# A four-layer graph network on one core: layers 1 and 2 computed over half the columns at a time, and the end of layer 0 moved behind the branch, block by block

## The chip, the cores and the metric

The kernel runs on one core of one Trainium2 chip. The metric is the device time of one execution in microseconds (us). A core has five engines that run their own instruction streams and wait for each other through semaphores: TensorE (PE in the profile; its weight loads are PEld), VectorE (DVE), ScalarE (ACT), GpSimd (POOL) and SyncE (SP), which here issues nearly all loads. Sixteen DMA engines move data between memory (HBM) and the on-chip memory SBUF. TensorE writes its results into PSUM, from where VectorE or ScalarE fetch them.

## The reference

There are N = 2708 nodes with D = 128 features, `x`, and one dense adjacency `adj` of 2708 x 2708 zeros and ones in float32, 29.3 MB. Four layers each take `h = max(layernorm(x), 0)` and add a graph operation to `x`. Cut to what matters:

```python
# layer 0: attention
H = h @ weight.T
Tau = adj.T * exp(max(0.2 * C, C))            # C[i, j] = alpha_src[j] + alpha_dst[i]
x = x + (adj.T * (Tau / Tau.sum(1))) @ H
# layer 1: normalised convolution
adj_hat = adj + eye(n);  d = (adj_hat.sum(1) + 1e-8) ** -0.5
x = x + relu((d[:, None] * adj_hat * d[None, :]) @ h @ weight)
# layer 2: mean aggregation, batch norm over all nodes
agg = adj.T @ h / deg
g = agg @ W_n.T + b_n + h @ W_c.T + b_c
x = x + relu(gamma * (g - g.mean(0)) * rsqrt(g.var(0) + 1e-5) + beta)
# layer 3: two products with adj around an attention of low rank
```

Layers 1 and 2 are each, in the main, one product of the whole adjacency with a 2708 x 128 matrix. In layer 2 the mean and variance over all nodes must be known before the layer can be added to `x`.

## The kernel before

**Tiling.** The 2708 nodes make T = 22 tiles of 128 rows (the last has 20), and the columns of the adjacency make NB = 6 blocks of 512 (the last has 148), listed in `E0`; `TILES[b]` gives the four row tiles that correspond to block b. `xs`, `hn`, `hs` hold node features by tiles; `hT` and `yT` hold a features-by-nodes matrix; `row_a`, `row_b` and `dflat` (two times N wide) are large scratch rows, [128, N] each.

**Layer 0** (up to L394) runs over the 22 row tiles of `adj`. After the loop come the flag (L362 to L368), the denominators `rden`, and a loop over the six blocks (L380 on): the last two tiles' matmuls, `evacuate` of the accumulator into `hT`, transposes back to tiles, an addition into `xs`, and `layernorm(b, hn, dis)`, which makes layer 1's input `hn`. `layernorm` takes statistics on VectorE, a power -0.5 on GpSimd (L165), scale and shift on VectorE, and the rectified output on ScalarE (L183). During layer 0, at `t == T - 4`, the first two row tiles of `adj_t` for layer 1 are loaded into `dflat`.

**The branch.** The flag tells whether all inputs of the adjacency have empty low halves. Each engine reads it and goes into one of two copies of `rest(exact, stack3)`; here it is `exact=True`. Whatever stands ahead of the branch is finished by an engine before it goes in. At the head of `rest` GpSimd writes the reciprocal degrees `rdeg` to DRAM element by element (L464) and reads them back spread over all partitions into `row_a` (L465), which layer 2's end uses.

**Exact products.** A float32 operand goes to TensorE in the format F32R. The features are cut into a high and a low part, `h_hi` and `h_lo` (`cut_in_two`, L481 and L482), so each adjacency row tile is used by two matmuls per block. The row tile itself is copied once to F32R (L503) by ScalarE or VectorE, into the pool `ring` (four whole rows).

**`loader`** hands out row tiles: load i goes into the buffer `turn[i % len(turn)]`. Layer 1 has five whole-row buffers (two halves of `dflat`, `row_b`, `hT`, and one of pool `raws`), layer 2 has four (`dflat` twice, `hn`, `raws`). A load can be issued when the copy to `ring` that last read its buffer is done; SP issues in order.

**`product`** runs one layer: for each of the first 18 row tiles, all six blocks are accumulated in six PSUM banks (`aggregate`, L216, 12 matmuls a tile); the last four tiles are loaded and worked off block by block, with `finish` behind each block. Layer 1's `finish1` takes one block out of PSUM, multiplies by the weight (L534), rectifies (L536), adds into `xs` and runs `layernorm(b, h2)` and `cut_in_two(h2, b)`, where `h2` is layer 2's input. Layer 2's `finish2` makes the two products of the layer in float32 (L567, L568) and block statistics (`st2`, L570). During layer 2's first loads `load_with_turn` transposes `h2` block by block into `hT`. Behind the last block `bn_aggr` joins the statistics (L574), and layer 2's end and layer 3 follow.

The program says what depends on what; a scheduler puts the instructions of each engine in one order. `keep_in_program_order` ties the instructions that are marked with it to their order in the text.

Of the kernel before, what the change touches and what calls it, by code (L numbers as in the profile page):

```python
# [14 lines left out]
ALU = mybir.AluOpType  # L15
# [4 lines left out]
def kernel(  # L20
# [35 lines left out]
    TILES = [range(c // P, min(c // P + 4, T)) for c, _ in E0]  # L56
    CUT = 3 * 512

    NLAST = 4

    def rows(t):
        return min(P, N - t * P)

    def fill(a, src, t):

        if rows(t) < P:
            nc.gpsimd.memset(a, 0.0)
        nc.sync.dma_start(a[: rows(t), :], src[t * P : t * P + rows(t), :])
        return a

    def cols(t):
# [13 lines left out]
    def bank():  # L85
        return ps.tile([P, 512], F32, tag="bank", name="bank")
# [100 lines left out]
    def turned(p, src, tiles, flat=None):  # L187

        for q, t in enumerate(tiles):
            nc.tensor.transpose(p[:, cols(q)], src[:, cols(t)] if flat else src[:, t, :], ident)  # L190
# [19 lines left out]

    def aggregate(stationary, moving, accs, start, stop, blocks=range(NB)):
        parts = stationary if isinstance(stationary, list) else [stationary]
        for b in blocks:
            lo, hi = E0[b]
            for i, w in enumerate(parts):
                nc.tensor.matmul(  # L216
                    accs[b][:, : hi - lo],
                    w,
                    moving[:, lo:hi],
                    start=start and i == 0,  # L220
                    stop=stop and i == len(parts) - 1,
                )

    def product(order, stationary, load, blocks, finish, extra=None):

        accs = [acc_bank(b) for b in range(NB)]
        for i, t in enumerate(order[:-NLAST]):
            a = load(t)
            aggregate(stationary(t), a, accs, i == 0, False)
            if extra:  # L230
                extra(t, accs)
        last = [(t, load(t)) for t in order[-NLAST:]]
        for b in blocks:
            for t, a in last:
                if extra and t in TILES[b]:
                    extra(t, accs)
                aggregate(stationary(t), a, accs, False, t == order[-1], [b])
            finish(b, accs[b])

    with ExitStack() as stack:  # L240
# [72 lines left out]
        for t in range(T):  # L313
            a = first_rows[t] if t < 3 else load_rows(adj, t)
            late = t >= T - 2
            rhs = (yT, row_b)[t % 2]
            for h, (h0, h1) in enumerate(((0, CUT), (CUT, N))):
                w = h1 - h0
# [32 lines left out]
            if t == T - 4:  # L351

                for i in range(2):
                    fill(dflat[:, i * N : (i + 1) * N], adj_t, i)
            if t == 10:
# [104 lines left out]
    def rest(exact, stack3):  # L460
# [26 lines left out]
        def loader(src, fixed, there=0):  # L487

            turn = [*fixed, raws] + ([] if exact else [ring] * NLAST)
            count = [0]  # L490

            def load(t):
                i = count[0]
                count[0] += 1
                a = turn[i % len(turn)]
                if a is raws or a is ring:
                    a = a.tile([P, N], F32, tag="rows", name="rows")
                if i >= there:
                    fill(a, src, t)
# [3 lines left out]
                m = nc.scalar.copy(r, a) if i % 2 else nc.vector.tensor_copy(r, a)  # L503
# [8 lines left out]
        def load_plus_one(t):  # L512
            a = next_row(t)
            if not exact:
                r = rows(t)
                nc.vector.tensor_add(a[:r, vcols(t)], a[:r, vcols(t)], ident[:r, :r])
            return a

        def plus_one(t, accs):

            r = rows(t)
            o = t % 4 * P
            for part_h in halves_of(hn)(t):
                nc.tensor.matmul(accs[t // 4][:, o : o + r], part_h, ident_r[:, :r], start=False, stop=False)

        for b in range(NB):
            cut_in_two(hn, b)
        def finish1(b, acc):
            evacuate(b, yT, acc)
# [19 lines left out]
        tot = small.tile([P, 8], F32, tag="tot", name="tot", bufs=1)  # L549
        turns = list(range(NB))  # L550

        next_row2 = loader(adj, [*two, hn.rearrange("p t d -> p (t d)")[:, :N]])

        def load_with_turn(t):
            a = next_row2(t)
            if turns:
                b = turns.pop(0)
# [3 lines left out]
            return a  # L561

# [700 lines left out]
```

## Time and profile before

| | |
|---|---|
| median of 3 runs | 898.41 us (897.56 to 898.52) |
| profiled execution | span 898.0 us, 8549 instructions, mean TensorE clock 0.922 of full speed |
| PE busy | 743.5 us (83%) |
| DVE busy | 581.6 us (65%) |
| ACT busy | 529.0 us (59%) |
| POOL busy | 194.6 us (22%) |
| DMA | 218.57 MB, mean 243 GB/s over the span |
| layer 0 | start to about 200 us |
| layer 1, first to last aggregation matmul | 234.8 to 322 us |
| layer 2, first aggregation matmul to `bn_aggr` | 335.6 to 409.7 us |

A line of a timeline gives start, length, engine, line and operation, what is written from what, its shape, how many in a row, and in brackets how long the engine sat idle before it and what released it ("issue": nothing that the profile shows). A line of a table of stretches gives the stretch, its length, the busy time of PE, PEld, DVE, ACT and POOL with the number of instructions, the granted TensorE clock (1.00 is full), the mean busy share of the 16 DMA engines and the GB/s that they moved. A line of the chain gives start, length and the piece of work that was waited for.

### The profile page before, as it was taken

The numbers are of one execution on the slowest core, as the hardware profiler recorded it, in microseconds if no ns is written. First come the engines' busy times: TensorE is split into PE (matmuls) and PEld (weight loads), VectorE is DVE, ScalarE is ACT, GpSimd is POOL, SyncE is SP. The second block draws the span as 40 slices with busy tenths as digits, with TensorE's granted clock in tenths as the row PEclk, the third lists the DMA queues.
The fourth block names the chain that finished last, engine by engine and source line by source line (L and its number), as shares of the span: only waits on it lengthen the run. The fifth ranks groups of instructions, "written<-read, shape, count | busy, mean of one in ns | idle before, by whom it ended". The sixth has DMA issues, their size and how long they took to land.

```text
span 898.0 us, 8549 instructions
## 1 busy us (share of the span) xinstructions
PE 743.5 (83%) x2980; PEld 430.8 (48%) x2980; DVE 581.6 (65%) x1079; ACT 529.0 (59%) x569; POOL 194.6 (22%) x159
## 2 busy tenths in 40 slices
PE   3599999991578869887767988389999999989996
PEld 2333333330466747764422322255555555545784
DVE  5599888885422472236886987366676666764844
ACT  3999999984234463345791015277777877766100
POOL 3000000022001020011100011365666666620010
PEclk9799999995699969997887999589999999999999
DMA  8154645404599929976510893576777777785993
GB/s 324 63 186 161 234 176 180 178 10 162 112 424 395 357 113 406 422 296 270 173 56 1 344 415 128 214 282 249 281 287 277 270 264 267 276 306 220 419 421 121
DMA packets 33394, 218.57 MB, mean 243 GB/s; under 512 B 4458, under 2 KB 13338, under 8 KB 13866
## 3 DMA queue, kind: packets, MB, share of 16 engines
q1 hardware_dynamic: 21596, 150.19, 43.5%
q0 software_dynamic: 8656, 65.76, 20.2%
q10 hardware_dynamic: 3090, 1.99, 0.7%
q8 instruction: 26, 0.43, 0.2%
q14 instruction: 26, 0.21, 0.1%
HBM read 214.12 MB, written 3.79 MB: 243 GB/s over the span
## 4 chain that ended last, share of the span: by engine, by line
DMA 22%; PE 19%; DVE 13%; POOL 7%; issue 7%; ACT 6%; DVEq 0%; POOLq 0%; ACTq 0%
DMA dflat<-in_adj_t_dram 6%; DMA dflat<-in_adj_dram 6%; PE bank L1141 5%; DMA hs<-in_adj_t_dram 4%; PE acc L1085 3%; PE acc L760 3%; PE acc L216 3%; DMA row_b<-pre_d,pre_i 2%; DMA yT<-pre_d,pre_i 2%; ACT rows L1103 2%; DVE rows L503 2%; POOL hs L597 2%; POOL hT L597 2%; PE bank L1031 1%; POOL row_b L597 1%
## 5 line engine op out<-in xcount | busy, mean ns | idle before, releaser
L1141 PE MATMUL bank<-rows,d_hi 128*128 128x512 f32 (+1 forms) x264 | 108.3, 414 | 36.9 <-DVE d_hi L1110 17.4
L216 PE MATMUL acc<-rows,h_hi 128*128 128x512 f32 (+1 forms) x264 | 104.2, 400 | 31.5 <-DVE rows L503 21.6
L1085 PE MATMUL acc<-e,xw 128*128 128x512 f32 (+1 forms) x264 | 104.3, 545 | 0.0
L1146 ACT ACTIVATE ln<-bank,tiny 128x512 f32<-128x512 f32 x132 | 79.9, 633 | 34.8 <-PE bank L1141 34.8
L1141 PE MATMUL bank<-rows,d_lo 128*128 128x512 f32 (+1 forms) x264 | 100.4, 391 | 0.0
L216 PE MATMUL acc<-rows,h_lo 128*128 128x512 f32 (+1 forms) x264 | 97.4, 386 | 0.0
L1141 PEld LDWEIGHTS bank<-rows,d_hi 128*128 128x128 f32 x264 | 52.6, 199 | 65.3 <-ACT ln L1146 29.4
L1149 DVE TENSOR_TENSOR e<-e,ln 128x1536 f32<-128x1536 f32 (+2 forms) x66 | 69.7, 1096 | 20.1 <-ACT ln L1146 19.9
L324 DVE SCALAR_TENSOR_TENSOR tau<-tau,e_hi,a 128x1536 f32<-128x1536 f32 (+1 forms) x44 | 70.6, 1622 | 7.3 <-DMA a<-in_adj_dram 5.0
L216 PEld LDWEIGHTS acc<-rows,h_hi 128*128 128x128 f32 x264 | 51.8, 197 | 45.7 <-DVE rows L503 22.6
L1085 PEld LDWEIGHTS acc<-e,xw 128*128 128x128 f32 x264 | 48.4, 190 | 52.6 <-issue 52.6
L321 ACT ACTIVATE tau<-row_a,e_neg,e_lo 128x1536 f32<-128x1536 f32 (+1 forms) x44 | 65.7, 1505 | 2.9 <-PE bank L333 2.7
L333 PE MATMUL bank<-tau,ones_at 128*32 128x512 f32 (+1 forms) x264 | 53.0, 567 | 8.3 <-DVE tau L324 8.3
L216 PEld LDWEIGHTS acc<-rows,h_lo 128*128 128x128 f32 x264 | 51.8, 196 | 10.8 <-issue 1.0
L1155 ACT ACTIVATE e<-e 128x2708 f32<-128x2708 f32 x22 | 54.2, 2462 | 4.2 <-DVE e L1149 4.2
L503 ACT CAST rows<-dflat 128x2708 fp32r<-128x2708 f32 x11 | 27.0, 2452 | 50.0 <-DMA dflat<-in_adj_t_dram 28.3
L1141 PEld LDWEIGHTS bank<-rows,d_lo 128*128 128x128 f32 x264 | 52.7, 200 | 7.4
L216 PE MATMUL acc<-yT,hs 128*128 128x512 f32 x132 | 56.3, 560 | 0.0
L216 PE MATMUL acc<-row_b,hs 128*128 128x512 f32 x132 | 56.1, 558 | 0.0
L216 PE MATMUL acc<-rows,y_hi 128*128 128x512 f32 x132 | 49.3, 380 | 5.2 <-DVE rows L1218 3.3
L503 DVE CAST rows<-dflat 128x2708 fp32r<-128x2708 f32 x11 | 17.3, 1570 | 54.5 <-DMA dflat<-in_adj_t_dram 30.3
L216 PE MATMUL acc<-rows,y_lo 128*128 128x512 f32 x132 | 47.7, 376 | 0.0
(406 smaller groups left out, 1404.2 us busy)
## 6 DMA issues: line engine op xcount, KB each, us to landing
a<-in_adj_dram SPq DMA_DIRECT2D x21, 1354.0 KB
rows<-in_adj_t_dram SPq DMA_DIRECT2D x21, 1354.0 KB
dflat<-in_adj_t_dram SPq DMA_DIRECT2D x15, 1354.0 KB
dflat<-in_adj_dram SPq DMA_DIRECT2D x11, 1354.0 KB
hT<-in_adj_t_dram SPq DMA_DIRECT2D x9, 1354.0 KB
row_b<-in_adj_t_dram SPq DMA_DIRECT2D x8, 1354.0 KB
hn<-in_adj_dram SPq DMA_DIRECT2D x5, 1354.0 KB
rows<-in_adj_dram SPq DMA_DIRECT2D x5, 1354.0 KB
```

The source lines that it names most:

```text
L216: nc.tensor.matmul(accs[b][:, : hi - lo], w, moving[:, lo:hi], start=start and i == 0, stop=stop and i == len(parts) - 1,)
L321: nc.scalar.activation(tau[:, :w], row_a[:, h0:h1], AF.Relu, bias=e_neg[:, t : t + 1], scale=e_lo[:, t : t + 1])
L324: nc.vector.scalar_tensor_tensor(tau[:, :w], tau[:, :w], e_hi[:, t : t + 1], a[:, h0:h1], ALU.add, ALU.mult)
L333: nc.tensor.matmul(den[g : g + 32, : hi - lo], ones_at[:, b // GR, :], tau[:, lo - h0 : hi - h0], start=(t == 0 and b < GR), stop=(t == T ...
L503: m = nc.scalar.copy(r, a) if i % 2 else nc.vector.tensor_copy(r, a)
L597: return nc.gpsimd.indirect_dma_start(out=out, out_offset=None, in_=src, in_offset=bass.IndirectOffsetOnAxis(ap=idx, axis=0),)
L760: nc.tensor.matmul(accs[b][64 * h : 64 * h + 2 * NC, : hi - lo], wts[:r, t, :], a[:r, lo:hi], start=(t == 0), stop=(t == T - 1),)
L1085: m = nc.tensor.matmul(accs[b][:, : hi - lo], xw, e[:, lo:hi], start=(s == 0), stop=(s == NE - 1))
L1141: m = nc.tensor.matmul(num[:, : hi - lo], d, a[:, lo:hi], start=(i == 0), stop=(i == len(products) - 1))
L1146: nc.scalar.activation(ln[:, lo:hi], num[:, : hi - lo], AF.Ln, bias=tiny)
L1149: tc.keep_in_program_order(nc.vector.tensor_sub(e[:, beg:hi], e[:, beg:hi], ln[:, beg:hi]))
L1155: tc.keep_in_program_order(nc.scalar.activation(e, e, AF.Exp))
```

## The change

Layers 1 and 2 go over the columns in two passes, `COLS`: blocks 0 to 2 (1536 columns), then blocks 3 to 5 (1172 columns). `product_by_halves` takes the place of `product` for both: in each pass it loads the half rows of all 22 tiles, accumulates three blocks, and finishes the three blocks behind the last four tiles. Both layers take the tiles in plain order. Loads are `fill_half`, each marked to stay in program order. Layer 1 has eight half-row buffers (three in `dflat`, one in `row_b`, four in `raws`), layer 2 also eight (`hn` in place of `row_b`); `ring` has six half rows. `hT` is no longer a load buffer in layer 1. Three half rows of `adj_t` are loaded during layer 0.

Of layer 0's last loop only the matmuls and `evacuate` stay ahead of the branch. The transposes, the addition, the layernorm and the cut of a block are now `finish0(b)`, behind the branch: block 0 ahead of layer 1's product, blocks 1 to 5 called with the loads of tiles 0, 4, 8, 12 and 16 of the first pass. `rden` moves to a pool that lives on. The cut of `h2` for blocks 0 to 2 is called in layer 1's second pass (after the loads 5, 9 and 13), for block 3 and for blocks 4 and 5 in `finish1`. The transposes of `h2` are called in layer 2 after loads 2, 4 and 6 of each pass. The copies to `ring` alternate between ScalarE and VectorE as before, except that loads 0 to 4 of a layer all go to ScalarE.

```diff
+    COLS = ((0, CUT), (CUT, N))
...
+    def fill_half(a, src, t, h):
+
+        if rows(t) < P:
+            nc.gpsimd.memset(a, 0.0)
+        tc.keep_in_program_order(
+            nc.sync.dma_start(a[: rows(t), :], src[t * P : t * P + rows(t), slice(*COLS[h])])
+        )
...
+    def product_by_halves(order, stationary, load, finish, extra, after):
+
+        for h, (h0, _) in enumerate(COLS):
+            blocks = range(3 * h, 3 * h + 3)
+            accs = {b: acc_bank(b) for b in blocks}
+            for i, t in enumerate(order[:-NLAST]):
+                a = load(t, h)
+                aggregate(stationary(t), a, accs, i == 0, False, blocks, h0)
+                if t // 4 in blocks:
+                    extra(t, accs)
+                after(i, h)
+            last = [(t, load(t, h)) for t in order[-NLAST:]]
+            for b in blocks:
+                for t, a in last:
+                    if t in TILES[b]:
+                        extra(t, accs)
+                    aggregate(stationary(t), a, accs, False, t == order[-1], [b], h0)
+                finish(b, accs[b])
...
-                for i in range(2):
-                    fill(dflat[:, i * N : (i + 1) * N], adj_t, i)
+                for i in range(3):
+                    fill_half(dflat[:, i * CUT : (i + 1) * CUT], adj_t, i, 0)
...
-        rden = small.tile([P, 4, GR, NB // GR], F32, tag="rden", name="rden", bufs=1)
+        rden = const.tile([P, 4, GR, NB // GR], F32, name="rden")
...
             evacuate(b, hT, accs[b])
-            p = bank()
-            turned(p, hT, TILES[b], True)
-            for q, t in enumerate(TILES[b]):
-                r = rows(t)
-                nc.vector.scalar_tensor_tensor(
-                    xs[:r, t, :], p[:r, cols(q)], rden[:r, q, b % GR, b // GR : b // GR + 1], xs[:r, t, :], ALU.mult, ALU.add
-                )
-            layernorm(b, hn, dis)
...
-        ring = s12.enter_context(tc.tile_pool(name="ring", bufs=NLAST))
-        raws = s12.enter_context(tc.tile_pool(name="raws", bufs=1))
+        ring = s12.enter_context(tc.tile_pool(name="ring", bufs=6))
+        raws = s12.enter_context(tc.tile_pool(name="raws", bufs=4))
...
-                r = ring.tile([P, N], F32R, tag="rows", name="rows")
-                m = nc.scalar.copy(r, a) if i % 2 else nc.vector.tensor_copy(r, a)
+                r = ring.tile([P, CUT], F32R, tag="rows", name="rows")[:, :w]
+                m = nc.vector.tensor_copy(r, a) if i % 2 and i > 4 else nc.scalar.copy(r, a)
...
-        two = [dflat[:, :N], dflat[:, N : 2 * N]]
-        next_row = loader(adj_t, [*two, row_b[:, :N], hT[:, :N]], 2)
+        three = [dflat[:, i * CUT : (i + 1) * CUT] for i in range(3)]
+        next_row = loader(adj_t, [*three, row_b[:, :CUT]], 3)
...
+            a = next_row(t, h)
+            if h == 0 and t % 4 == 0 and t // 4 + 1 < NB:
+                finish0(t // 4 + 1)
...
+        def finish0(b):
+
+            p = bank()
+            turned(p, hT, TILES[b], True)
+            for q, t in enumerate(TILES[b]):
+                r = rows(t)
+                nc.vector.scalar_tensor_tensor(
+                    xs[:r, t, :], p[:r, cols(q)], rden[:r, q, b % GR, b // GR : b // GR + 1], xs[:r, t, :], ALU.mult, ALU.add
+                )
+            layernorm(b, hn, dis)
             cut_in_two(hn, b)
+
+        finish0(0)
...
-            cut_in_two(h2, b)
-
-        order1 = [*range(12), *range(16, T), *range(12, 16)]
-        product(order1, halves_of(hn), load_plus_one, [4, 5, 0, 1, 2, 3], finish1, plus_one if exact else None)
+
+            for o in {3: (3,), 5: (4, 5)}.get(b, ()):
+                cut_in_two(h2, o)
+
+        def after1(i, h):
+
+            if h == 1 and i in (5, 9, 13):
+                cut_in_two(h2, i // 4 - 1)
+
+        product_by_halves(range(T), halves_of(hn), load_plus_one, finish1, plus_one, after1)
...
-        next_row2 = loader(adj, [*two, hn.rearrange("p t d -> p (t d)")[:, :N]])
...
-        order2 = [TF - 2, TF - 1] + list(range(TF - 2)) + [TF]
-        product(order2, halves_of(h2), load_with_turn, range(NB), finish2)
+        next_row = loader(adj, [*three, hn.rearrange("p t d -> p (t d)")[:, :CUT]])
+        product_by_halves(range(T), halves_of(h2), next_row, finish2, lambda t, accs: None, turn)
```

More of the change, by code (lines that the diff above doesn't have):

```diff
@@ L209, in evacuate, with aggregate @@
             nc.scalar.copy(dst[:, lo:hi], acc[:, : hi - lo])
-    def aggregate(stationary, moving, accs, start, stop, blocks=range(NB)):
+    def aggregate(stationary, moving, accs, start, stop, blocks=range(NB), at=0):
         parts = stationary if isinstance(stationary, list) else [stationary]
@@ L218, in aggregate @@
                     w,
-                    moving[:, lo:hi],
+                    moving[:, lo - at : hi - at],
                     start=start and i == 0,
@@ L316 @@
             rhs = (yT, row_b)[t % 2]
-            for h, (h0, h1) in enumerate(((0, CUT), (CUT, N))):
+            for h, (h0, h1) in enumerate(COLS):
                 w = h1 - h0
@@ L487, in loader, with load @@
         def loader(src, fixed, there=0):
-            turn = [*fixed, raws] + ([] if exact else [ring] * NLAST)
+            turn = [*fixed] + [raws] * 4 + ([] if exact else [ring] * 6)
             count = [0]
-            def load(t):
+            def load(t, h):
                 i = count[0]
                 count[0] += 1
+                w = COLS[h][1] - COLS[h][0]
                 a = turn[i % len(turn)]
                 if a is raws or a is ring:
-                    a = a.tile([P, N], F32, tag="rows", name="rows")
+                    a = a.tile([P, CUT], F32, tag="rows", name="rows")
+                a = a[:, :w]
                 if i >= there:
-                    fill(a, src, t)
+                    fill_half(a, src, t, h)
                 if not exact:
                     return a
-                r = ring.tile([P, N], F32R, tag="rows", name="rows")
-                m = nc.scalar.copy(r, a) if i % 2 else nc.vector.tensor_copy(r, a)
+                r = ring.tile([P, CUT], F32R, tag="rows", name="rows")[:, :w]
+                m = nc.vector.tensor_copy(r, a) if i % 2 and i > 4 else nc.scalar.copy(r, a)
                 tc.keep_in_program_order(m)
@@ L507, in loader, with load_plus_one @@
             return load
-        two = [dflat[:, :N], dflat[:, N : 2 * N]]
-        next_row = loader(adj_t, [*two, row_b[:, :N], hT[:, :N]], 2)
[L512 to L516, printed above, removed]
+        three = [dflat[:, i * CUT : (i + 1) * CUT] for i in range(3)]
+        next_row = loader(adj_t, [*three, row_b[:, :CUT]], 3)
+        def load_plus_one(t, h):
+            a = next_row(t, h)
+            if h == 0 and t % 4 == 0 and t // 4 + 1 < NB:
+                finish0(t // 4 + 1)
+            if not exact and t // 4 // 3 == h:
+                r, c = rows(t), t * P - COLS[h][0]
+                nc.vector.tensor_add(a[:r, c : c + r], a[:r, c : c + r], ident[:r, :r])
             return a
@@ L522, in plus_one @@
             o = t % 4 * P
-            for part_h in halves_of(hn)(t):
-                nc.tensor.matmul(accs[t // 4][:, o : o + r], part_h, ident_r[:, :r], start=False, stop=False)
-        for b in range(NB):
+            if exact:
+                for part_h in halves_of(hn)(t):
+                    nc.tensor.matmul(accs[t // 4][:, o : o + r], part_h, ident_r[:, :r], start=False, stop=False)
+        def finish0(b):
[7 more added lines that the diff above has]
+            layernorm(b, hn, dis)
             cut_in_two(hn, b)
+        finish0(0)
         def finish1(b, acc):
@@ L549, in rest, with turn @@
         tot = small.tile([P, 8], F32, tag="tot", name="tot", bufs=1)
-        turns = list(range(NB))
-        next_row2 = loader(adj, [*two, hn.rearrange("p t d -> p (t d)")[:, :N]])
[L554 to L557, printed above, removed]
+        def turn(i, h):
+            if i in (2, 4, 6):
+                b = 3 * h + i // 2 - 1
                 p = bank()
@@ L560, in load_with_turn @@
                 nc.vector.tensor_copy(hT[:, spans(b)], p[:, : len(TILES[b]) * P])
-            return a
         def finish2(b, acc):
```

## The prediction

> **What bounds the kernel now.** I read the page's slices first, to see where the DMA engines and TensorE rest, then a table of stretches around layers 1 and 2, then the order of work at the edges of those stretches. From the page, the 40 slices (22.45 us each):
>
> ```profile
> PE   3599999991578869887767988389999999989996
> PEclk9799999995699969997887999589999999999999
> DMA  8154645404599929976510893576777777785993
> GB/s 324 63 186 161 234 176 180 178 10 162 112 424 395 357 113 406 422 296 270 173 56 1 344 415 128 214 282 249 281 287 277 270 264 267 276 306 220 419 421 121
> ```
>
> Slices 9 to 17 (202 to 404 us) hold the end of layer 0, the branch, layer 1 and layer 2. Inside layer 1 (slices 11 to 13) and layer 2 (15 to 17) the DMA engines move some 400 GB/s and are never idle: these layers are bound by loading the adjacency once each. Slices 9, 10 and 14 move a quarter of that. The stretches make it exact (us, busy time and count of each engine, clock, DMA share, GB/s):
>
> ```profile
> 199.00:204.00 5.00, 3.15 (x23) 2.15 (x21) 3.65 (x20) 0.59 (x1) 0.73 (x1) 1.00 0.01 2
> 204.00:221.00 17.00, 2.89 (x10) 1.72 (x10) 11.12 (x72) 8.24 (x20) 5.73 (x6) 0.52 0.36 126
> 221.00:234.80 13.80, 0.00 (x0) 0.00 (x0) 7.14 (x16) 6.96 (x5) 1.61 (x1) 0.50 0.48 155
> 234.80:244.00 9.20, 9.18 (x36) 7.55 (x37) 3.09 (x3) 0.00 (x0) 0.60 (x1) 0.78 0.62 72
> 244.00:300.00 56.00, 47.79 (x238) 39.39 (x237) 11.96 (x8) 19.62 (x8) 2.36 (x1) 1.00 1.01 410
> 300.00:320.00 20.00, 16.96 (x86) 14.07 (x85) 10.98 (x42) 11.27 (x28) 3.05 (x3) 0.85 0.90 348
> 320.00:338.00 18.00, 10.69 (x39) 7.22 (x38) 13.78 (x45) 12.19 (x22) 3.58 (x3) 0.69 0.08 21
> 338.00:391.00 53.00, 48.22 (x213) 38.56 (x212) 13.70 (x9) 18.95 (x8) 2.36 (x1) 0.97 1.00 418
> 391.00:410.00 19.00, 17.50 (x62) 10.32 (x60) 9.57 (x24) 6.97 (x8) 0.07 (x1) 1.00 0.48 173
> ```
>
> Three holes: 204 to 244 (layer 0's six-block end, then the branch, then the cut of hn), 320 to 338 (layer 1's six-block end before layer 2 may start) and 391 to 410 (six-block end of layer 2). The timeline of TensorE, GpSimd and VectorE, and two pieces of the chain, show the first hole's edges:
>
> ```profile
> 216.93 0.69 PE L190 MATMUL bank<-ident,hT 128*128 128x128 f32 x2 [6.70 <-DVE hT L207]
> 234.82 0.80 PE L216 MATMUL acc<-rows,h_hi 128*128 128x512 f32 x1 [17.21 <-DVE rows L503]
> ```
> ```profile
> 226.51 1.61 POOL L464 DMA_DIRECT2D rdeg_d<-rdeg  x1 [5.76 <-issue]
> 242.00 0.60 POOL L465 DMA_DIRECT2D row_a<-rdeg_d  x1 [13.88 <-DMA rdeg_d<-rdeg]
> ```
> ```profile
> 227.79 0.34 DVE L475 CAST ident_r<-ident 128x128 fp32r<-128x128 f32 x1 [6.66 <-issue]
> ```
> ```profile
> 234.79 13.78 DMA dflat<-in_adj_t_dram
> ```
>
> Each engine passes the branch by itself (SP already loads at 204.10, while VectorE ends layer 0 at 221.13), and the branch costs it 5.8 us on GpSimd and 6.7 us on VectorE. The scatter of rdeg by single elements is issued at 226.51 and has landed 14.9 us later; the load issued at 234.79 needs 13.78 us, and the stretch 234.8 to 244 moves 72 GB/s: until the scatter is through, row loads hardly move.
>
> **The Trainium skill.** "Runtime: NRT & Kernel Launch", Instruction fetch mechanics: a taken branch out of the fetched pages must fetch its target before going on. The trace agrees in kind: 5.8 and 6.7 us of idle time with no releaser. "DMA: Bandwidth & Descriptors", Specifications: pieces under 512 B are read, modified and written; the 11 KB scatter's 14.9 us agree, though the page gives no time for it. Same section: 435 GB/s at most between memory and SBUF; the trace's 410 to 418 in the full stretches is near it, so no more is to be had there. "TensorE: Matmul & The Clock Gate", the HAM clock gate: half rate after some 3.4 us without work. The trace agrees: PEclk is 0.50 at 221 to 234.8 and 1.00 from 244 on, with TensorE busy 47.8 of 56 us.
>
> **The change, part by part.**
>
> *1. Layer 0's end behind the branch.* VectorE's last work before the branch becomes the evacuations, some 201.7 us (the row of L207 at 200.74 takes 0.68, one short copy of 0.28 follows). Plus 6.66: VectorE is through at 208.4. Then for block 0: ident_r 0.34, four additions 1.12 (row of L388), statistics 1.3, GpSimd 1.01, two small operations 0.3, four ACT 1.65, h_hi 0.4: 6.1 us, and waits between engines of some 1 us. TensorE starts at about 215.5 instead of 234.8. Block by block the rest costs VectorE 3.3 us (the pitch of blocks at 205 to 218) and 1.0 for the cut, 4.3 us; four half tiles take 7.5 us of loading, so blocks 1 to 5 hide behind loads. What queues behind their waits on VectorE are its casts of every second half row, 0.9 us each.
>
> *2. But the end is set by loads.* All bytes: 2 x 2708 rows x 10,832 B = 58.67 MB, plus row_a 1.39. Ahead of the branch three half tiles are loaded (3 x 128 x 6,144 B = 2.36 MB), before it was two whole ones (2.77). SP is at 204.1 as now, and five more half tiles wait on no engine's later work. Now GpSimd, too, is early: its last work before the branch ends at 199.7, the flag is there at 200.8, plus 5.76 gives 206.6 for the scatter, which the diff doesn't move in the text. In the trace free flow begins at 244.3, 17.8 us after the scatter's issue. The same distance gives **224.4**. Until then: 205.7 to 208.3 at full rate 1.1 MB, and some 0.8 MB through the scatter (72 GB/s x 11 us of it).
>
> The scatter is the unknown. It may cost nothing if the loads in the queue pass it (free flow from 205.7), and up to this. I take the full price, because the trace has the one case in which both were in flight and the load lost.
>
> *3. Half rows.* A 10,832 B packet took 407 ns in the trace's packet records, a 5,416 B one (pre_d) 208 ns: 9 ns each plus 0.0367 ns per byte. A row in two pieces of 6,144 and 4,688 B takes 416, +2.2%. Sustained rate before: 410 and 418; after, 414/1.022 = 405 GB/s. SP issues twice as many loads, 88 x 0.33 us = 29 us in some 155, hidden. Eight half buffers equal four whole ones; layer 2 ran at 418 GB/s with four. Four zero-fills of the short tile (2.36 us now, 1.4 for half) come in the middle of SP's queue, with three or more loads in flight: nothing. Casts: 44 more instructions, ACT 1.4 and VectorE 0.9 us against 1.9 us per load, alternating: hidden. Matmuls stay 264 pairs a layer.
>
> *4. The joint between the layers.* Layer 1's blocks 0 to 2 end beside its second half of loads; blocks 3 to 5 beside layer 2's first, whose stationary tiles 0 to 11 are ready. From 300 to 338 now 20 x 348 + 18 x 21 GB/s = 7.34 MB; at 410 they take 17.9 us. **20.1 us** saved. One bound: layer 2's first load takes dflat, whose cast is layer 1's fourth from last: three loads in flight, 4.3 us of work, so no gap.
>
> *5. The sum.* Bytes left at 224.4: 58.67 + 1.39 - 2.36 - 1.9 = 55.8 MB, at 405 GB/s 137.8 us: the last lands at 363 (with 0.8 of completion). Before: 393.0.
>
> *6. The tail.* From the last landing to bn_aggr's end now 393.0 to 409.7, 16.6 us, six blocks. After: cast 0.8, two matmuls 0.5, blocks 4 and 5 of four tiles 1.9 + 0.7, three blocks' fp32 products 1.9 + 1.9 + 0.8, ACT and statistics 1.0, waits 1: **10.5 us**.
>
> So bn_aggr ends at 373.5 instead of 409.7: **36 us**; all behind it (rank, layer 3) moves along unchanged. 898.0 - 36 = 862; the other runs lie at 897.6 to 898.5, the median at 898.4, so 862 holds for them.
>
> *TensorE as second bound.* Tile pitch in the timeline: 2.76 us in layer 1, 2.54 in layer 2; 22 x (2.76 + 2.54) = 117. Transposes and block ends 20, a cold start 2: 139. From 215.5 that ends at 354, plus what it starves during the scatter (some 6): 360, before 373.5. It has 13 us to spare.
>
> **The rivals.**
>
> *A, the scatter doesn't hold the loads.* Flow from 205.7: 57.7 MB / 405 = 142.5, last landing 349, plus 10.5: 359.5, which is also TensorE's bound: 898 - 50 + 3 for two bounds that meet = 851. For: two different queues; against: 72 GB/s from 234.8 to 244.
>
> *B, the joints stall TensorE.* Now the six block ends of layer 1 take from 305.6 (first evacuation) to 335.6 (first matmul of layer 2), 5 us a block. If engines' orders keep three blocks in line at both of layer 1's joints, 30 us of idle TensorE: 215.5 + 139 + 30 = 384.5, saved 25: 873. For: VectorE and ACT do casts and block ends in one line. Against: now nothing else was ready to run at that joint; after the change the next half's matmuls are.
>
> *C, slower: TensorE stays at half clock.* With a gap after each half tile it could be granted 0.5: 0.43 us instead of 0.23 per 512-column matmul (pitch at 235 to 239), so 139 becomes some 250 and layer 2 ends at 465, kernel 953. It decides from a mean clock below 139 / (409.7 - 215.5) = 0.71. Against: from 247 to 270 it was busy 18.2 of 23 us, with gaps, at 1.00.
>
> *D, the split leaves the layers in line* (the compiler orders the halves' ends ahead of the next loads): only the early start counts. It is 19.9 us earlier with 3.3 MB less moved, 8.2 us, minus 2.9 for half rows: 9 us, 889.
>
> **How the numbers follow.** Main case 0.55 (854 to 868), A 0.20 (846 to 854), B 0.14 (868 to 880), D 0.05, C 0.04, no difference 0.02 (0.2% is about what a measurement can tell from nothing). The time is the main case's, **862**. 846 to 877 holds main, A and most of B: 0.55 + 0.20 + 0.09 = 0.84. Faster by over 0.2%: 0.94, within 0.02, slower 0.04.
>
> **What would show it.** Right: TensorE's first h_hi matmul near 215; GB/s near 400 from about 224 without a slice below 300 until the last load of layer 2; no hole at the joint; bn_aggr some 10 us after the last landing. The scatter's step is wrong if rows flow at 400 GB/s between 208 and 222. B is right if DMA shares fall under 0.9 with idle TensorE waiting for ACT or VectorE at the joints; C if PEclk is near 0.5 between 225 and 360. The prediction falls if layers 1 and 2 keep their length.

## The result: 886.2 us, a third of the gain that was forecast

| | median us (range) | ratio to before, 95% interval |
|---|---|---|
| before | 898.46 (897.56 to 900.06) | |
| changed | 886.21 (884.95 to 886.64) | 0.9859 [0.9842, 0.9877] |

The change makes the kernel 12.3 us faster. The forecast was 36 us, 862 with 846 to 877 as the range: the sign was right, the size was not. The profiled execution of the changed kernel has a span of 883.1 us; bn_aggr, the last operation of layer 2, ends at 395.56 us where it ended at 409.66 before (14.1 us earlier; 373.5 was forecast). From there to the end it is 487.5 us, before 488.3, so all of the miss lies ahead of 395.56.

### The profile after

The page's slices of the changed kernel, 22.08 us each: busy tenths of TensorE, its clock, the DMA share, and GB/s.

```profile
PE   3599999992695979987759986389999999989996
PEclk9799999995796979997679998689999999999999
DMA  8053455707996959996501985477777777785994
GB/s 328 2 190 135 180 189 189 296 11 117 336 394 235 366 207 407 374 381 248 192 0 64 389 326 195 171 290 279 280 269 268 266 267 265 273 319 221 417 427 141
```

The forecast wanted no slice under 300 from 224 us until layer 2's last load. Counted from 0 as in the prediction, slices 12 (265 to 287 us, 235 GB/s) and 14 (309 to 331 us, 207 GB/s) break that, and in both the clock drops with TensorE's idle time. The stretches say where. After the window come busy time and count of each engine, clock, DMA share and GB/s.

```profile
208.00:224.00 16.00, 1.11 (x4) 0.71 (x4) 2.27 (x16) 0.00 (x0) 2.63 (x3) 0.50 0.99 161
224.00:260.00 36.00, 32.35 (x143) 26.47 (x144) 21.04 (x73) 25.98 (x35) 5.33 (x5) 0.88 0.97 365
260.00:270.00 10.00, 7.52 (x45) 6.25 (x43) 4.88 (x15) 5.50 (x15) 0.00 (x0) 0.99 0.96 391
270.00:280.00 10.00, 1.53 (x4) 1.24 (x5) 4.84 (x24) 7.59 (x15) 3.02 (x3) 0.50 0.29 72
280.00:310.00 30.00, 29.52 (x157) 25.04 (x156) 11.59 (x24) 11.65 (x14) 1.08 (x1) 0.94 0.97 369
310.00:330.00 20.00, 13.82 (x50) 9.29 (x49) 9.92 (x32) 13.10 (x22) 2.71 (x3) 0.74 0.52 192
330.00:370.00 40.00, 37.64 (x165) 28.50 (x163) 14.93 (x20) 18.69 (x16) 1.38 (x1) 1.00 0.98 385
370.00:387.00 17.00, 17.00 (x86) 13.71 (x85) 4.87 (x7) 6.46 (x6) 1.08 (x1) 1.00 0.97 382
```

There are three holes. **208 to 224**: the DMA engines are busy 0.99 of the time and move 161 GB/s, so they are slow, not idle. **270 to 280** (layer 1's joint between its two halves of columns) and **310 to 330** (the joint between layers 1 and 2): here the DMA share itself falls to 0.29 and 0.52, so the engines have nothing to do. The sum: from 224 to 387 the rows above hold 54.6 MB, which at the forecast's 405 GB/s take 134.8 us; they took 163. Of the 28.2 us that are missing, 8.2 lie in 270 to 280 (10 x (405 - 72) / 405) and 10.5 in 310 to 330, worked out alike; 3.6 in 224 to 260 and 6.0 in the rest, where the rate is 369 to 391.

The first hole in the timelines of GpSimd, VectorE, ScalarE and TensorE (start, duration, engine, line, operation, and in brackets the idle time before it and what ended it):

```profile
204.67 1.61 POOL L484 DMA_DIRECT2D rdeg_d<-rdeg  x1 [3.46 <-issue]
221.12 0.60 POOL L485 DMA_DIRECT2D row_a<-rdeg_d  x1 [14.84 <-DMA rdeg_d<-rdeg]
221.75 2.02 POOL L174 TENSOR_TENSOR rstd<-isq,neg_half 128x4 f32<-128x4 f32 x2
```
```profile
204.43 0.23 DVE L495 CAST ident_r<-ident 128x128 fp32r<-128x128 f32 x1 [4.13 <-issue]
222.81 0.16 DVE L189 TENSOR_TENSOR rstd<-rstd,dis 128x4 f32<-128x4 f32 x1 [12.90 <-POOL rstd L174]
```
```profile
224.33 1.65 ACT L192 ACTIVATE hn<-xs,shift,rstd 128x128 f32<-128x128 f32 x4 [18.95 <-DVE shift L190]
225.88 1.46 ACT L525 CAST rows<-dflat 128x1536 fp32r<-128x1536 f32 x1
```
```profile
227.39 0.80 PE L225 MATMUL acc<-rows,h_hi 128*128 128x512 f32 x1 [1.93 <-ACT rows L525]
```

VectorE passes the branch at 204.4, 4 us ahead of the forecast's 208.4. But the powers that finish block 0 (L174) stand on GpSimd's queue behind row_a's read (L485), and that waits 14.84 us for the scatter (L484). VectorE then waits 12.90 us for the power, ScalarE 18.95, and TensorE starts at 227.4 instead of 215.5.

The second hole, the joint inside layer 1, in the timelines of ScalarE, TensorE and SP's DMA queue:

```profile
275.71 1.65 ACT L192 ACTIVATE hs<-xs,shift,rstd 128x128 f32<-128x128 f32 x4 [0.32 <-DVE shift L190]
277.27 1.15 ACT L525 CAST rows<-rows 128x1172 fp32r<-128x1172 f32 x1
278.32 2.23 ACT L525 CAST rows<-dflat 128x1172 fp32r<-128x1172 f32 x2
```
```profile
266.76 1.16 PE L571 MATMUL bank<-w_sb,yT 128*128 128x128 f32 x8 [0.40 <-ACT o L573]
278.47 0.79 PE L225 MATMUL acc<-rows,h_hi 128*128 128x512 f32 x1 [10.55 <-ACT rows L525]
```
```profile
261.04 17.73 SPq L77 DMA_DIRECT2D rows<-in_adj_t_dram  x4
279.51 1.40 SPq L77 DMA_DIRECT2D dflat<-in_adj_t_dram  x3
```

ScalarE's first cast of the next half follows directly behind the last layer norm of the blocks before it. TensorE idles 10.55 us for it. SP's four loads stretch over 17.73 us, as their buffers come free only when the casts have read them. The joint between the layers has the same look, in the timelines of ScalarE and TensorE:

```profile
321.83 0.88 ACT L192 ACTIVATE hs<-xs,shift,rstd 128x128 f32<-128x128 f32 x2 [0.20 <-DVE shift L190]
322.61 4.21 ACT L525 CAST rows<-dflat 128x1536 fp32r<-128x1536 f32 x3
```
```profile
324.12 0.79 PE L225 MATMUL acc<-rows,h_hi 128*128 128x512 f32 x1 [1.57 <-ACT rows L525]
```

Layer 2 has such a joint between its own two halves of columns, too, but it costs little: from 350 to 370 us the changed kernel moves 382 and then 333 GB/s, some 2.3 us of loading short of 405.

### The profile page after: what moved, and what is told of

The parts are those of the page before. It is cut to its first block, busy times and chain, and to the rows that moved or that the text cites. A ratio compares the mean times of both kernels' runs of the same rounds, so it can differ in the third digit from the quotient of the medians.

```text
span 883.1 us, 8728 instructions
## 1 busy us (share of the span) xinstructions
PE 739.1 (84%) x2980; PEld 428.5 (49%) x2980; DVE 580.9 (66%) x1097; ACT 536.9 (61%) x595; POOL 196.0 (22%) x161
## 4 chain that ended last, share of the span: by engine, by line
PE 14%; DMA 11%; DVE 9%; POOL 7%; issue 7%; ACT 5%; POOLq 0%; DVEq 0%; ACTq 0%
DMA hs<-in_adj_t_dram 4%; PE acc L797 3%; PE bank L1178 3%; PE acc L1122 2%; DMA row_b<-pre_d,pre_i 2%; DMA yT<-pre_d,pre_i 2%; POOL hs L634 2%; ACT rows L1140 2%; PE acc L225 2%; POOL hT L634 2%; PE bank L1068 1%; DVE bits L731 1%; POOL yT L634 1%; POOL row_b L634 1%; POOL xw L634 1%
## 5 line engine op out<-in xcount | busy, mean ns | idle before, releaser
L225 PE MATMUL acc<-yT,hs 128*128 128x512 f32 x132 | 55.8, 560 | 0.0
L525 ACT CAST rows<-dflat 128x1536 fp32r<-128x1536 f32 (+1 forms) x26 | 34.2, 1332 | 24.9 <-DMA dflat<-in_adj_dram 13.9
L1161 DVE TENSOR_SCALAR xw<-xw,c_exp 128x128 f32<-128x128 f32 x22 | 6.6, 298 | 57.8 <-DMA xw<-xw_d,xw_i 57.8
```

Of the source, the lines that this page charges most:

```text
L225: nc.tensor.matmul(accs[b][:, : hi - lo], w, moving[:, lo - at : hi - at], start=start and i == 0, stop=stop and i == len(parts) - 1,)
L525: m = nc.vector.tensor_copy(r, a) if i % 2 and i > 4 else nc.scalar.copy(r, a)
```

## The experiments

My theory after this result had two parts. First, the scatter of rdeg holds row loads until 224 us and thereby sets the end. Second, at both joints the casts of the next half stand in line behind block ends, because `tc.keep_in_program_order(m)` keeps each cast at its written place in its engine's order, which is behind them. All runs, with the end of bn_aggr in the profiled execution of each; e1 to e4, e5 to e8 and e9 to e11 ran as three sets, in which the kernel before had medians of 899.6, 899.0 and 901.0, so that across sets the ratios are compared:

| kernel | median us (range) | ratio to before | bn_aggr ends |
|---|---|---|---|
| e1 row_a's read later | 887.59 (884.62 to 888.10) | 0.9861 [0.9807, 0.9915] | 395.8 |
| e2 flat write | 876.32 (875.05 to 877.13) | 0.9749 [0.9699, 0.9800] | 384.6 |
| e3 free casts | 873.18 (868.07 to 874.96) | 0.9698 [0.9637, 0.9759] | 383.7 |
| e4 halves only | 896.00 (892.53 to 899.88) | 0.9962 [0.9942, 0.9982] | 407.6 |
| e5 moved end only | 891.97 (888.12 to 893.46) | 0.9923 [0.9895, 0.9952] | 402.5 |
| e6 flat write, free casts | 857.19 (856.42 to 858.13) | 0.9537 [0.9513, 0.9561] | 369.8 |
| e7 e6, row_a's read later | 859.15 (855.35 to 863.80) | 0.9579 [0.9542, 0.9616] | 370.9 |
| e8 before, flat write | 887.75 (886.06 to 892.63) | 0.9874 [0.9846, 0.9902] | 400.5 |
| e9 e6, joint inside layer 1 tied | 862.94 (859.31 to 865.59) | 0.9585 [0.9536, 0.9634] | 375.6 |
| e10 e6, joint between layers tied | 865.21 (864.25 to 867.41) | 0.9609 [0.9570, 0.9648] | 378.2 |
| e11 e6, two half tiles ahead | 859.27 (857.09 to 862.19) | 0.9538 [0.9494, 0.9582] | 370.7 |

### The start: GpSimd's queue or the scatter (e1, e2)

**e1** takes row_a's read off the head of GpSimd's queue.

```diff
-        nc.gpsimd.dma_start(row_a[:, :N], rdeg_d[:N].partition_broadcast(P))
...
+            if h == 0 and t == 20:
+                tc.keep_in_program_order(
+                    nc.gpsimd.dma_start(row_a[:, :N], rdeg_d[:N].partition_broadcast(P))
+                )
```

> The read of the reciprocal degrees into row_a is moved from the head of GpSimd's queue to behind the power operations of layer 0's end; the scatter stays where it is. Theory 'loads' (the scatter holds the row loads until about 222 us whatever GpSimd does; the block on GpSimd only adds the hole at 228 to 236 us, where loads wait for late copies): TensorE's first h_hi matmul moves from 227.4 to about 215 us, but the kernel gains only 3 to 5 us over the changed one, about 882. Rival 'late start' (TensorE's late start is what was lost): it gains the whole 12 us, about 874.

Neither number came: 887.6 us, no gain. In its trace GpSimd's first power starts at 208.66 and TensorE's first h_hi matmul at 214.42, 13 us earlier than in the changed kernel and within 1.1 us of the forecast's 215.5. But it has only the half tiles loaded so far, and then waits. The timelines of ScalarE and TensorE, and a stretch:

```profile
226.24 1.47 ACT L524 CAST rows<-rows 128x1536 fp32r<-128x1536 f32 x1 [6.02 <-DMA rows<-in_adj_t_dram]
```
```profile
227.76 0.79 PE L225 MATMUL acc<-rows,h_hi 128*128 128x512 f32 x1 [4.58 <-ACT rows L524]
```
```profile
208.00:224.00 16.00, 9.88 (x43) 7.83 (x42) 12.26 (x70) 8.78 (x12) 4.93 (x5) 0.73 0.96 72
```

From 208 to 224 it moves 72 GB/s. So TensorE's late start alone is not worth the 12 us that the rival expects, which lie outside e1's interval. The 3 to 5 us of the other expectation are within its noise, and the traces show where they may have gone. From 224 to 260 e1 moves 404 GB/s against 365 in the changed kernel, 1.4 MB more; but from 200 to 224 it moves 75 against 146, 1.7 MB less, as its first load starts 0.8 us later and its loads are held until 224 instead of 222. The loads of e3 start 2.5 us later, though its edit doesn't touch this place, so shifts of that size may come from one execution to the next.

**e2** leaves that wait where it is and changes what the scatter writes: TensorE turns the 128 x 22 reciprocals first, so that the same 11 KB go out as 22 rows of 512 bytes in place of single elements.

```diff
+        turn_d = bank()
+        nc.tensor.transpose(turn_d[:T, :P], rdeg, ident)
+        rdeg_t = const.tile([T, P], F32, name="rdeg_t")
+        nc.vector.tensor_copy(rdeg_t, turn_d[:T, :P])
...
-        nc.gpsimd.dma_start(rdeg_d.rearrange("(t p) -> p t", p=P), rdeg)
+        nc.gpsimd.dma_start(rdeg_d.rearrange("(t p) -> t p", p=P), rdeg_t)
```

> The reciprocal degrees are turned by TensorE ahead of the branch and written to DRAM as 22 rows of 512 B instead of 2816 single elements; the read into row_a stays at the head of GpSimd's queue. Theory 'loads': the write lands within 3 us, row loads run at some 400 GB/s from 206 us on, GpSimd is free at 208 instead of 221 us, and the kernel gains 10 to 13 us over the changed one, about 875. Rival (the scatter does not hold the loads): the only gain is GpSimd's early release, as in the run with the late read, 3 to 5 us, about 882.

It gives 876.3 us, 9.9 less than the changed kernel (0.9749 against 0.9859). The stretch and GpSimd's timeline:

```profile
208.00:224.00 16.00, 9.37 (x31) 7.01 (x32) 11.98 (x68) 10.45 (x15) 4.88 (x6) 0.56 1.01 388
```
```profile
205.01 0.77 POOL L488 DMA_DIRECT2D rdeg_d<-rdeg_t  x1 [3.56 <-DVE bias L594]
210.34 0.60 POOL L489 DMA_DIRECT2D row_a<-rdeg_d  x1 [4.55 <-DVE xs L561]
```

388 GB/s from 208 to 224 against 161: 16 x 0.227 = 3.6 MB more, 9.0 us of loading at 405 GB/s, of the 9.9 gained. GpSimd, too, goes on 11 us earlier, but e1 gained nothing that can be seen from that alone. So the scatter's form, not its place on GpSimd, sets the start.

### The joints: are the casts tied (e3)

```diff
-                tc.keep_in_program_order(m)
+                if src is adj_t and i < T:
+                    tc.keep_in_program_order(m)
```

Casts stay tied in layer 1's first half alone; at both joints they may take another place in their engine's order than the one written.

> The copies to the ring are tied to the order of the text only in layer 1's first pass; from there on the scheduler may put them between the block ends. Theory 'copies behind block ends' (at both joints of layer 1 the ring copies stand behind the layernorms of three blocks on ScalarE and VectorE, so buffers are not freed and loads stop): the holes at 270 to 280 and 310 to 330 us, worth 8.2 and 10.5 us of loading at 405 GB/s, shrink by half or more, 8 to 14 us, about 875. Rival (TensorE's own chain through the block ends makes the holes): under 3 us, about 885.

873.2 us, 13.0 less than the changed kernel (0.9698 against 0.9859). The joints' stretches:

```profile
260.00:280.00 20.00, 17.84 (x94) 14.90 (x93) 9.28 (x34) 12.26 (x24) 2.01 (x2) 0.99 0.98 382
280.00:310.00 30.00, 27.46 (x143) 23.21 (x141) 11.90 (x22) 14.55 (x21) 2.64 (x2) 0.89 0.90 325
310.00:330.00 20.00, 17.68 (x79) 12.67 (x79) 13.62 (x44) 17.35 (x27) 2.71 (x3) 1.00 1.00 401
```

The two holes (72 GB/s over 10 us, 192 over 20) are gone. From 280 to 310 it is now 325, where the changed kernel had 369, and why was not looked into. The edit frees the casts at layer 2's own joint as well, so that the 2.3 us there are a part of what it can gain. ScalarE's timeline shows the new order: the cast falls between the parts of a block end.

```profile
269.05 0.59 ACT L218 COPY yT<-acc 128x512 f32<-128x512 f32 x1 [2.68 <-PE acc L225]
269.53 1.17 ACT L525 CAST rows<-rows 128x1172 fp32r<-128x1172 f32 x1
270.60 0.59 ACT L218 COPY yT<-acc 128x512 f32<-128x512 f32 x1
```

### The two halves of the change by themselves (e4, e5)

e4 is the changed kernel with layer 0's six block ends ahead of the branch again (`finish0`'s body back in layer 0's loop). e5 is the kernel before with only that end moved behind the branch, at layer 1's whole rows 0, 2, 4, 6 and 8.

> Layer 0's end stands ahead of the branch again, as before; everything else of the change stays. Theory 'loads': scatter and free flow fall back to where they were before (244 us instead of 224), some 3 us of which is made up by loads that land ahead of the scatter, and the half rows by themselves gain the short tail (some 7 us) less their packets (3 us): 890 to 897. Rival (the halves make the gain and layer 0's end none): about 886, as the changed kernel.

> The kernel before with layer 0's end alone moved behind the branch, one block before each of layer 1's loads 0, 2, 4, 6 and 8, and rows still whole (with four load buffers in layer 1 in place of five, as hT is then still read). Theory (the moved end is where nearly all of the change's gain came from, since the halves alone gave 3.5 us): 886 to 890 us. Rival (with whole rows TensorE needs all six blocks' h_hi for its first tile's later matmuls at once and loads fill four buffers and stop, so the moved end gives nothing): 896 to 900 us.

896.0 and 892.0 us, e4 inside its range and e5 2 us over it. e4's gain is 0.38%, e5's 0.77%, and their sum 1.15% is near the change's 1.41%. One stretch of each:

```profile
228.00:244.00 16.00, 14.34 (x63) 11.78 (x62) 5.34 (x12) 7.12 (x6) 0.60 (x1) 0.88 0.56 64
```
```profile
310.00:330.00 20.00, 11.15 (x43) 7.55 (x42) 15.06 (x55) 12.61 (x25) 4.59 (x4) 0.63 0.14 49
```

The first is e4: with the end ahead of the branch the scatter's hold falls at 228 to 244 as it did before. The second is e5: whole rows keep the old hole between the layers. The halves shorten that one but bring a second: e4 moves 94 GB/s from 282 to 293, at the joint inside layer 1, and 79 from 326 to 338, at the one between the layers. So alone they gain next to nothing.

### Both mends, and the scatter in the kernel before (e6, e7, e8)

> The changed kernel with both mends: the reciprocals turned by TensorE and written as rows of 512 B, and the ring's copies tied to the written order in layer 1's first pass alone. Theory (two separate holes, one of the scatter at the start and one of copies tied behind block ends at the two joints, and the loads set the end in between): the gains add, 886.2 - 10 - 13 = 863 us, and no stretch of 10 us between 208 and 370 us under 250 GB/s. Rival (one later bound, TensorE's work, takes over as soon as either hole is closed): 870 to 874 us, no better than the free copies alone.

e6 has e2's and e3's edits together: **857.2 us**, 0.9537 [0.9513, 0.9561], the lowest median here (e7 and e11 can't be told from it), and it beats both kernels. The rival, one later bound at 870 to 874, is out. Its slices (21.41 us each), to be set beside the changed kernel's:

```profile
PE   3599999995898999967679792799999998989996
DMA  9044544724998999967106936777777777785994
GB/s 337 3 153 173 187 164 174 301 76 161 354 398 322 348 417 395 361 274 263 66 1 254 416 139 236 266 274 265 281 271 278 263 283 261 276 307 231 418 426 138
```

Slices 10 to 16 (214 to 364 us) lie between 322 and 417. If the two single gains add, the ratio is 0.9859 - 0.0110 - 0.0161 = 0.9588; e6 is 0.5% below that, and 6 us below the 863 expected. The intervals leave room for it (0.005 to 0.006 each side on e2 and e3), so I read nothing into it. That no stretch of 10 us would be under 250 GB/s held: the slowest 10 us between 208 and 370, from 263 to 273, move 260.

> As the kernel with both mends, and row_a's read moved on GpSimd's queue behind the powers of layer 0's blocks. Theory (with rows of 512 B the write lands in a few us, so the read no longer holds GpSimd's powers): within 2 us of the kernel with both mends, about 863 us. Rival (the read still stands ahead of the first powers for the 2 to 5 us between its issue and its landing, and TensorE's first half tiles wait for that): 858 to 860 us.

e7 adds e1's edit: 859.2, no gain. The 1.9 us by which TensorE starts earlier (215.97 against 217.89) are not seen at the end.

> The kernel before with the reciprocals' write alone as rows of 512 B. Theory (the scatter holds layer 1's loads in the kernel before as well, whose end is set by loads too): 5 to 11 us less than before, 888 to 894 us. Rival (in the kernel before the scatter's hold lies beside layer 0's end and costs nothing): 897 to 900 us.

e8 puts e2's edit alone into the kernel before: 887.8 us, 0.9874 [0.9846, 0.9902]. That is just under its range, and as much as the whole change brings. GpSimd's timeline and the stretch that answers to 64 GB/s in e4:

```profile
227.29 0.77 POOL L468 DMA_DIRECT2D rdeg_d<-rdeg_t  x1 [6.04 <-issue]
230.13 1.01 POOL L469 DMA_DIRECT2D row_a<-rdeg_d  x1 [2.06 <-DMA rdeg_d<-rdeg_t]
```
```profile
228.00:244.00 16.00, 8.77 (x35) 7.22 (x36) 10.05 (x17) 7.17 (x4) 1.08 (x2) 0.65 0.72 271
```

The wait for the write is 2.06 us where it was 13.88 in the kernel before. TensorE starts no earlier (235.24, before 234.82); 3.6 MB more are loaded by 244 (271 against 43 GB/s), 9 us, and bn_aggr ends 9.2 us earlier.

### One joint at a time, and loads further ahead (e9, e10, e11)

e9 and e10 are e6 with the condition of e3's edit changed, so that the casts are tied again at one joint.

e9, tied at the joint inside layer 1:

```diff
-                if src is adj_t and i < T:
+                if src is adj_t:
```

e10, tied at the joint between the layers:

```diff
-                if src is adj_t and i < T:
+                if src is adj or i < T:
```

> The changed kernel with the reciprocals' write as rows of 512 B, and the ring's copies left free in layer 2 alone (the joint between the layers; inside layer 1 they stay tied). Theory (each joint has its own hole, since each one's copies are tied behind its own block ends): about half of the 19 us between 876.3 and 857.2 comes back, 865 to 869 us, and the loads dip under 150 GB/s at 260 to 280 us but nowhere between 290 and 330 us. Rival (the hole at the joint between the layers is only the lateness of the first handed on): 874 to 877 us.

> The same, with the copies left free in layer 1's second pass alone (the joint inside layer 1; in layer 2 they stay tied). Theory: the other half, 865 to 869 us, with the dip left between 290 and 330 us alone. Rival: all of it, 857 to 860 us, as the second hole follows from the first.

862.9 and 865.2 us, e9 2 us under its range, e10 inside. Both rivals, where the second hole is only the first one handed on, are out: each joint has its own hole, and it stays where its casts are tied. It is the traces that show this for e9, since its interval overlaps e6's. The stretches 260 to 280 and 300 to 320 of e9, then of e10:

```profile
260.00:280.00 20.00, 9.78 (x38) 8.15 (x39) 8.95 (x35) 12.49 (x22) 3.02 (x3) 0.66 0.57 206
300.00:320.00 20.00, 19.62 (x102) 15.98 (x101) 13.78 (x43) 15.14 (x24) 2.71 (x3) 1.00 1.02 419
```
```profile
260.00:280.00 20.00, 15.28 (x61) 12.25 (x61) 8.94 (x32) 13.07 (x21) 3.07 (x3) 0.83 0.86 304
300.00:320.00 20.00, 15.49 (x56) 11.19 (x57) 9.93 (x28) 15.16 (x18) 2.47 (x3) 0.83 0.68 258
```

Between e2 (both tied, 0.9749) and e6 (none, 0.9537) lie 2.1% or 19 us. To free the joint between the layers alone gives 0.9749 - 0.9585 = 1.6% of it, to free the one inside layer 1 gives 1.4%: more than 2.1% together. So the holes are separate, and their gains overlap, by some 8 us at the middle of intervals of about half a per cent each, which is barely clear of the noise. (e9 and e10 also leave free or tie the casts at layer 2's own joint, together with the one between the layers.) What meets the gains may be TensorE; this is argued and not shown. Over the 130 us from 240 to 370 it is busy 110.0 in the changed kernel and 120.0 in e6, so that with both holes closed less of its idle time is left to fill.

> The kernel with both mends, and at each joint the next pass's first two half tiles loaded ahead of the last four tiles' block ends in the written order. Theory (what is left between 208 and 350 us is loads at 300 to 420 GB/s, TensorE busy 86 to 100% in most stretches, so little is left to gain): 853 to 858 us. Rival (the stretches at 300 GB/s round 270 and 285 us are SP's queue standing behind buffers that the joint holds): 848 to 852 us.

e11 loads two half tiles of the next pass ahead of the last block ends: 859.3 us, no gain, 1 us over its range and far from the rival's. The stretches that should have filled stay as they were (301 GB/s at 260 to 270, 298 at 280 to 290), so SP's order of loads is not what limits them; TensorE is busy 9.79 us in the latter.

## Why the prediction was wrong

The step that failed is the joint: step 4's "so no gap", and with it step 3's "hidden" for the casts. The forecast put both at nothing. In the changed kernel the casts stood in line behind the block ends, and that cost 18.7 us of loading, 8.2 inside layer 1 and 10.5 between the layers; with the casts freed (e3) the kernel takes 873.2, inside the forecast's range. A second term was mis-sized: the rate of 405 GB/s in step 3, which cost another 9.6 us.

The steps, one by one.

1. **Layer 0's end behind the branch**: wrong in its time, without an effect on the end that a run shows. The working took 1.01 us for GpSimd's power and did not look at what the power stands behind: row_a's read, 14.84 us. TensorE started at 227.4, not 215.5. e1, where it starts at 214.4, is no faster, though the 3.6 us that are missing from 224 to 260 go with the late start: e1 moves 404 GB/s there instead of 365.
2. **The scatter's hold**: right, and the full price was the right choice. Free flow was forecast from 224.4; it came at 222, with 396 GB/s to 224 and 415 from 224 to 228. e2 and e8 show that it is the single-element write which does it, and rival A (no hold) is out.
3. **Half rows**: a packet of 6,144 bytes takes 234 ns and one of 4,688 takes 181 in the packet records, 415 together against the 416 worked out. The sustained rate of 405 GB/s was reached only in parts: 404 and 419 from 330 to 350, but 365 to 391 in most, which is the 3.6 + 6.0 us above. The split itself allows the rate: e9 moves 419 from 300 to 320 with half rows. "Casts: ... hidden" failed. Their duration is hidden (1.2 to 1.5 us each on ScalarE, 0.8 on VectorE); their place in line was not looked at.
4. **The joint**: "three loads in flight, 4.3 us of work, so no gap" failed. The forecast counted bytes and buffers and took matmuls that had their stationary side as ready to run. Their moving side is the cast's output, and the cast was tied behind the block ends. The old hole between the layers, worth 20.1 us, went; 8.2 and 10.5 us came back at the two joints. e3, e9 and e10 show it by undoing it.
5. **The end of the loads**: forecast 363, measured 386.8. The 28.2 us of lost rate, less 3.0 for the 1.2 MB that had come in earlier than assumed (54.6 against 55.8 left), less the 0.8 of completion that the sum had added and the 0.4 from 224.0 to its start at 224.4, are 24.0 against the 23.8 measured.
6. **The tail**: forecast 10.5, measured 386.8 to 395.6, 8.8 us.

Of the rivals, the mechanism of **B** is what happened, engines' orders holding block ends and casts in one line, at both of the joints where it was put. It was sized as 30 us of idle TensorE on top of TensorE's own bound, which gave 873. In fact the lines cost 18.7 us of loads, and on top of the loads' bound that makes 862 + 18.7 = 880.7; with the lower rate elsewhere (9.6), the earlier bytes (-3.0), the completion and the start (-0.8, -0.4) and the shorter tail (-1.7) it is 884.4, between the span of 883.1 and the median of 886.2. What spoke against B in the text ("the next half's matmuls are") was wrong. C is out: TensorE's mean clock from 227.4 to 387 is 0.91, where C needed less than 0.71; it falls where TensorE idles and is 1.00 from 330 on. D's 889 is the nearest in time, and its picture half holds: inside layer 1 the three block ends are through before the second half's first cast runs on ScalarE. But it is the casts that stand in line, not the loads, which the compiler let through until their buffers were full; and D's 9 us for the early start alone is near the 7 that e5 measured.

With the casts free and the scatter's hold kept, as steps 2 and 4 had it, the kernel is e3, and it took 873: 11 us over the forecast. Most of them lie in two stretches: 280 to 310 at 325 GB/s is 5.9 us short of 405, 224 to 260 at 367 is 3.4 us short. That 857 with both mends lies so near to 862 is chance: e6 has the free start that the forecast did not assume.

## What to carry to other kernels

When work is let overlap, follow every operand of the instruction that should fill the gap back through its engine's queue: a copy that is short and looks hidden can stand behind exactly the work that it should run beside. Look also at the smallest transfers at a stage's edge: 11 KB written as single elements cost as much time as the whole change here gained. And before a wait is removed, ask what stands behind it: e1 and e7 let TensorE start 13 and 2 us earlier, and no gain could be seen.

## What the hardware showed that was not expected

- The write of 2,816 single elements holds the loads of another queue for most of its flight: 161, 72 and 94 GB/s from 208 to 224 us in the changed kernel, e1 and e3, against 388 and 379 in e2 and e6, where it goes out in rows of 512 bytes. The changed kernel's slowest part is 212 to 222, with 63 to 97 GB/s. In its packet records 42 of the write's own 48 packets start before 212, and they take 62 or 81 ns in the median, by size; but the 135 load packets of 6,144 bytes that start between 212 and 222 take 1.02 us on average, against the usual 234 ns. So it is the loads' own packets that are drawn out, after nearly all of the write's have been worked off. The Trainium skill ("DMA: Bandwidth & Descriptors", Specifications) says that pieces under 512 bytes are read, modified and written; the direction agrees, but that row says nothing of other queues. The wait for the write fell from 13.88 us to 2.06 with the queues otherwise as in the kernel before. Whether memory or the DMA engines' own handling draws the loads out was not tried.
- The branch cost VectorE 4.13 us and GpSimd 3.46 in the changed kernel, where the kernel before showed 6.66 and 5.76 at the same place: taking the figure over from one kernel to another is good to some 2.5 us.
